# Eight unused columns behind each block of the sign weights

## The chip, the cores and the metric

The kernel runs on one core of a Trainium2 chip. The metric is the device time of one execution in microseconds; the time before is the median of three runs, 437.38 us (437.32 to 437.59).

## The reference

The input x is 2 sequences of 4096 vectors of 256 (fp32). A gated recurrence comes first, then a feed-forward layer with binarised weights; each is added to its input and followed by a layer norm.

```python
u = x @ W_in + b_in                       # 64 wide
g = sigmoid(x @ W_gate + b_gate)          # 256 wide
h_t = tanh(h_prev @ A + u_t @ Bm)         # a scan over 4096 steps
y_t = h_t @ C.T + u_t @ D.T
y_t = g_t * y_t + (1.0 - g_t) * x_t
x1 = layernorm(x + ys @ W_out + b_out + x)

alpha = mean(abs(w), axis=1, keepdims=True); bw = alpha * sign(w)
f = gelu(einsum('bsd,hd->bsh', x1, bw1) + b1)     # 1024 wide
out = layernorm(x1 + einsum('bsh,dh->bsd', f, bw2) + b2)
```

What matters here is the second half: both of its weight matrices are a sign (-1, 0 or 1) times one scale per row. The kernel multiplies by the signs alone and applies the scales afterwards.

## The kernel before, in words

The 8192 tokens are 16 chunks of 512 (`N`). The scan is cut into 64 segments that run side by side (`SEG`), so that a step of the recurrence is one small product `ps_s` (L157) and a tanh for all segments; these steps are strewn among the other work. The order of instructions on every engine is written out by hand (`manual_schedule`), and a running sum of costs (`emit`, `COST`) decides where a step of the recurrence is put in. The first 80 us or so hold the recurrence's input `u` (L131) and the first gates `ps_g` (L313); then comes the loop over chunks. In one round of the loop a chunk goes through its four `up` and four `down` parts, while chunks after it go through the gate, the mix `ps_y` (L374), the projection `ps_z` (L399) and the turning, and the chunk before it through the last layer norm.

The products that concern the change are two.

- `up` (L486): `ps_h`, 128 of the 1024 hidden units for 512 tokens. The weights that are loaded are a block of `sg1`, 128 columns for one of the two halves `k` of the 256 inputs and one of the eight blocks `j`; the moving operand is x1, split in two fp32r parts, `xhi` and `xlo`, of which each is 512 columns. Four matmuls make one `ps_h`, in the order (xhi, k=0), (xhi, k=1), (xlo, k=0), (xlo, k=1), all with the same j. There are 512 in a run.
- `down` (L528): `ps_o`, 128 tokens by 256 outputs. Here the loaded weights are 128 columns of the hidden layer, split into `hhi` and `hlo`, and the moving operand is block j of `sg2`, 256 columns. For one j there are eight matmuls in a row (four blocks of tokens, two parts). There are 1024 in a run, in the last chunk partly under the name `ps_p`.

Both are fp32r, one pass each. The other products are fp32: the trace shows two instructions for each of them. In the trace each matmul has a record of the weight load (PEld) and one of the product (PE).

`sg1` and `sg2` are made once, early in the kernel: `load_w` brings in the weights in four parts, `prepare_w` reduces them to scales, and `signs` writes the signs, on VectorE, with a comparison (L194) and a combination (L195) for each 512 columns. `signs` takes flat rows before the change. All tiles of the pool `const`, and then those of the other pools, lie one behind another in each partition, in the order in which they are asked for, so the sizes of `sg1` and `sg2` move what lies behind.

Of the kernel before, what the change touches and what calls it, by code (L numbers as in the profile page):

```python
# [8 lines left out]
FP = mybir.dt.float32  # L9
FR = mybir.dt.float32r  # L10
I32 = mybir.dt.int32
AF = mybir.ActivationFunctionType
ALU = mybir.AluOpType
# [3 lines left out]
P = 128  # L17
B, T, DM, S, H = 2, 4096, 256, 64, 1024
KD = DM // P
KH = H // P  # L20
# [3 lines left out]
N = 512  # L24
# [5 lines left out]
TOL = 2.0**-20  # L30
TGB = 9
XTB = 8
EARLY = 500
TOP, LOW = slice(0, S), slice(S, P)

# [2 lines left out]
def gated_recurrence_then_binary_ffn(  # L38
# [16 lines left out]
    nc = tc.nc  # L55

    cp = ctx.enter_context(tc.tile_pool(name="const", bufs=1))
    xp = ctx.enter_context(tc.tile_pool(name="xin", bufs=2))
    wk = ctx.enter_context(tc.tile_pool(name="work", bufs=2))
# [16 lines left out]
    cd = cp.tile([P, DM], FP, name="cd")  # L76
    w_gate = cp.tile([P, KD, DM], FP, name="w_gate")
    w_out = cp.tile([P, KD, DM], FP, name="w_out")
    sg1 = cp.tile([P, KD, H], FR, name="sg1")
    sg2 = cp.tile([P, KH, DM], FR, name="sg2")  # L80
    bias_c = cp.tile([P, 1 + KD + KH], FP, name="bias_c")
    bin_c = bias_c[:, 0:1]
    b1_c = bias_c[:, 1 + KD :]
# [16 lines left out]
    def load_xT(c, pieces=1):  # L100
        x_tiles[c] = xp.tile([P, KD, N], FP, tag="xt", name=f"xt{c}", bufs=XTB)
        for k in range(pieces):
            cut = slice(k * KD // pieces, (k + 1) * KD // pieces)
            nc.sync.dma_start(out=x_tiles[c][:, cut, :], in_=xT[c][:, cut, :])
# [19 lines left out]
    def u_of_chunks(*chunks):  # L124

        n = N * len(chunks) // 2
        parts = [(chunks[0], 0), (chunks[1], 0) if len(chunks) == 2 else (chunks[0], 1)]
        ps = p_1.tile([P, N], FP, tag="h", name=f"ps_u{chunks[0]}")
        for k in range(KD):
            for (c, i), r in zip(parts, (LOW, TOP)):  # L130
                nc.tensor.matmul(  # L131
                    ps[r, :n],
                    w_in[k],
                    x_tiles[c][:, k, bass.ts(i, n)],
                    start=k == 0,
                    stop=k == KD - 1,
                    skip_group_check=True,
                )
        for (c, i), r in zip(parts, (LOW, TOP)):
            to = u_of[:, bass.ds(c * SPC + i * n // W, n // W)].rearrange("p j b k -> p (j b k)")  # L140
            if r is TOP and c == FIRST:
                nc.scalar.activation(to, ps[r, :n], AF.Identity, bias=bin_c[r, :])
            else:
                nc.vector.tensor_scalar(to, ps[r, :n], bin_c[r, :], None, ALU.add)
        have_u.update(chunks)
        yield
# [42 lines left out]

    def signs(dst, src, nm):  # L190

        for i in range(2):
            neg = wk.tile([P, N], FP, tag="xlo", name=f"neg{nm}_{i}")
            nc.vector.tensor_scalar(neg, src[:, bass.ts(i, N)], 0.0, None, ALU.is_lt)  # L194
            nc.vector.scalar_tensor_tensor(  # L195
                dst[:, bass.ts(i, N)], src[:, bass.ts(i, N)], 0.0, neg, ALU.is_gt, ALU.subtract
            )

    w_tiles = {}
# [14 lines left out]
    def prepare_w(n):  # L214
        half = bass.ts(n % 2, KH // 2)
        t, t2 = w_tiles[n]
        if n < 2:
            nc.vector.tensor_reduce(al1[:, half], t2, AX.X, ALU.add, apply_absolute_value=True)
            nc.vector.tensor_scalar(al1[:, half], al1[:, half], 1.0 / DM, None, ALU.mult)
            signs(sg1[:, n, :], t, f"a{n}")  # L220
        else:
            nc.vector.tensor_reduce(
                al2[:, n % 2, :],
                t.rearrange("p j d -> p d j"),
                AX.X,
                ALU.add,
                apply_absolute_value=True,
            )
            if n == 3:
                nc.vector.tensor_add(al2[:, 0, :], al2[:, 0, :], al2[:, 1, :])  # L230
            signs(
                sg2[:, half, :].rearrange("p j d -> p (j d)"),
                t.rearrange("p j d -> p (j d)"),
                f"b{n}",
            )

    def mean_w2():
        ps = p_1.tile([P, N], FP, tag="h", name="ps_al2")
# [90 lines left out]
    class Chunk:  # L329
# [6 lines left out]
        def load_x(self):  # L336
            self.xt = xp.tile([P, KD, N], FP, tag="xt", name=f"xt_{self.nm}", bufs=XTB)
            nc.sync.dma_start(out=self.xt, in_=self.at(xT, self.c))
# [138 lines left out]
        def up(self, g, apart=False):  # L477
            nm = f"{self.nm}_{g}"
            h = wk.tile([P, 2, N], FP, tag="h", name=f"h{nm}")
            hi = wk.tile([P, 2, N], FR, tag="hhi", name=f"hhi{nm}", bufs=3)  # L480
            self.h[g] = h, hi
            for i in range(2):
                j = 2 * g + i
                ps = p_1.tile([P, N], FP, tag="h", name=f"ps_h{nm}_{i}")
                for n, (k, part) in enumerate((k, p) for p in (self.hi, self.lo) for k in range(KD)):
                    nc.tensor.matmul(  # L486
                        ps,
                        sg1[:, k, bass.ts(j, P)],
                        part[:, k, :],
                        start=n == 0,  # L490
                        stop=n == 2 * KD - 1,
                    )
                to = h[:, i, :]
                if self.far:
                    to = to.rearrange("p (i a c) -> p a i c", a=P // 32, c=32)
                nc.scalar.activation(  # L496
                    to,
                    ps.rearrange("p (a i c) -> p a i c", a=P // 32, c=32) if self.far else ps,
                    AF.Gelu,
                    bias=b1_c[:, j : j + 1],  # L500
                    scale=al1[:, j : j + 1],
                )
                if i == 1:
                    for part in range(2) if apart else [slice(0, 2)]:
                        nc.scalar.copy(hi[:, part, :], h[:, part, :])  # L505
                yield
# [18 lines left out]
        def down_part(self, j, tb):  # L525
            ps, i, first = self.banks[tb]
            for part in self.h[j // 2]:
                nc.tensor.matmul(  # L528
                    ps[:, i, :],
                    part[:, j % 2, bass.ts(tb, P)],  # L530
                    sg2[:, j, :],
                    start=j == 0 and part is self.h[j // 2][0] and first,
                    stop=j == KH - 1 and part is self.h[j // 2][1],
                    skip_group_check=True,
                )
# [128 lines left out]
    def emit(what, pieces, pace=5600):  # L664
        nonlocal since
        for _ in pieces:
            since += COST.get(what, 0)
            if since >= pace:
                since = min(since - pace, pace // 2)
                if ready():  # L670
                    next_steps()
# [21 lines left out]
    def parts(n, pace):  # L693
        emit("part", (next(early, None) for _ in range(n)), pace)

    ET = mybir.EngineType
    with tc.manual_schedule(engines={ET.PE, ET.Activation, ET.DVE, ET.Pool, ET.SP}):
# [8 lines left out]
        for n, pair in enumerate(pairs):  # L706
            before = 2 if n == 0 else 1
            parts(before, EARLY)
            if pair:
                emit("", u_of_chunks(*pair))  # L710
                if pair == (13, 14):
                    emit("", u_of_chunks(15, 0))
                emit("u", [None], EARLY)
            for c in loads[n]:
                load_xT(c)
            if n == 0:
                load_weights()
            if n == 3:
                halve_weights()
            if n >= 5:  # L720
                load_xT(n + 3)
                ch[n - 4].load_n()
                if n == 5:
                    ch[0].load_u()
                else:
                    ch[0].load_n()
                    ch[1].load_u()
                    ch[2].load_u()
            for i in range(7 - before):
                if 1 <= n < 5 and i == 0:  # L730
                    load_w(n - 1)
                if 2 <= n < 6 and i == 3:
                    prepare_w(n - 2)
                parts(1 if (n, i) != (6, 5) else 0, EARLY)
        assert done >= WARM + SPC, done
        emit("u", u_of_chunks(3), EARLY)
        for i in range(4):
# [191 lines left out]
```

## Time and profile before

| | |
|---|---|
| median of three runs | 437.38 us |
| the profiled execution | 437.67 us, its span 435.9 us |
| TensorE products (PE) | 425.5 us busy, 98% of the span, 2402 instructions |
| weight loads (PEld) | 344.3 us, 79% |
| VectorE | 332.4 us, 76% |
| ScalarE | 286.0 us, 66% |
| GpSimd | 155.8 us, 36% |
| `ps_h`, xhi and xlo | 256 + 256 matmuls, mean record 444 and 394 ns |
| `ps_o`, hhi and hlo | 496 + 496 matmuls, mean record 286 and 279 ns (32 more as `ps_p`) |
| granted TensorE clock | 0.994 of full speed |

A record of a matmul lasts from its start until its modelled end, and the records of neighbours overlap: the pace of TensorE is read from the distance between starts, or from the length of a piece in the chain of waits divided by its count, not from a record's length.

### The profile page before, as it was taken

What the parts mean: (1) busy time and instruction counts of PE and PEld (TensorE: products, weight loads), DVE (VectorE), ACT (ScalarE), POOL (GpSimd) and SP (SyncE); (2) the same over time, 40 slices, a digit from 0 to 9 for tenths busy, and PEclk for the clock granted to TensorE, in tenths of its full rate; (3) what the DMA queues carried; (4) which work ended last, traced back from release to release, by engine and by line L of the source; (5) the groups of instructions that cost most, each with busy time, mean ns of one, the idle gap of its engine ahead of it and who ended that gap; (6) DMA issues with size and microseconds to landing.
All of it is one profiled execution on the core that took longest, in us unless ns stands there. A gap on an engine that the chain in (4) does not pass through costs nothing.

```text
span 435.9 us, 6818 instructions
## 1 busy us (share of the span) xinstructions
PE 425.5 (98%) x2402; PEld 344.3 (79%) x2402; DVE 332.4 (76%) x569; ACT 286.0 (66%) x480; POOL 155.8 (36%) x176
## 2 busy tenths in 40 slices
PE   8999999999999999999999999999999999999992
PEld 5665767788888879797979797978888888888982
DVE  0245937895979798888888897979797979797674
ACT  2443452486587776767677776777767585849881
POOL 1000050474143435253525443444343444533413
PEclk9999999999999999999999999999999999999997
DMA  8877713400251615152426242534233232311102
GB/s 297 300 282 261 269 36 128 163 2 0 44 174 44 217 46 178 38 186 80 144 66 192 76 144 69 166 102 124 91 107 109 58 111 60 111 36 50 48 2 102
DMA packets 31479, 51.34 MB, mean 118 GB/s; under 512 B 5328, under 2 KB 19664, under 8 KB 31440
## 3 DMA queue, kind: packets, MB, share of 16 engines
q1 hardware_dynamic: 30864, 50.48, 36.4%
q8 instruction: 21, 0.34, 0.3%
q10 hardware_dynamic: 576, 0.37, 0.3%
q14 instruction: 18, 0.15, 0.1%
HBM read 31.43 MB, written 8.39 MB: 91 GB/s over the span
## 4 chain that ended last, share of the span: by engine, by line
PE 89%; DVE 5%; ACT 2%; DMA 1%; issue 1%; POOL 1%; SPq 0%; POOLq 0%; DVEq 0%
PE ps_h L486 25%; PE ps_o L528 25%; PE ps_g L313 12%; PE ps_z L399 11%; PE ps_y L374 6%; PE ps_s L157 6%; PE ps_u L131 3%; DMA xt<-in_xT 1%; DVE hlo L512 1%; ACT xn L278 1%; POOL rs_b L265 1%; PE ps_t L430 1%; DVE bs_b L255 1%; DVE d L381 1%; ACT h L496 1%
## 5 line engine op out<-in xcount | busy, mean ns | idle before, releaser
L528 PE MATMUL ps_o<-sg,hhi 128*128 128x256 f32 x496 | 121.4, 286 | 0.0
L528 PE MATMUL ps_o<-sg,hlo 128*128 128x256 f32 x496 | 117.9, 279 | 0.1
L496 ACT ACTIVATE h<-ps_h,bias_c,al 128x512 f32<-128x512 f32 x128 | 95.5, 771 | 16.8 <-PE ps_h L486 13.0
L528 PEld LDWEIGHTS ps_o<-sg,hhi 128*128 128x128 f32 x496 | 93.5, 189 | 1.1 <-DVE o L544 0.3
L528 PEld LDWEIGHTS ps_o<-sg,hlo 128*128 128x128 f32 x496 | 93.5, 188 | 1.1 <-DVE hlo L512 0.3
L486 PE MATMUL ps_h<-xhi,sg 128*128 128x512 f32 x256 | 92.9, 444 | 0.3 <-ACT h L496 0.3
L359 POOL TENSOR_TENSOR xn<-xn,bo_r 128x256 f32<-128x256 f32 x64 | 54.7, 888 | 88.6 <-DMA xn<-in_x 78.4
L512 DVE TENSOR_TENSOR hlo<-h,hhi 128x1024 fp32r<-128x1024 f32 (+1 forms) x65 | 79.5, 1240 | 5.0 <-ACT hhi L505 5.0
L486 PE MATMUL ps_h<-xlo,sg 128*128 128x512 f32 x256 | 80.1, 394 | 0.2
L265 POOL TENSOR_TENSOR rs_b<-rs_b,neg_half 128x4 f32<-128x4 f32 (+1 forms) x17 | 28.1, 1655 | 115.1 <-DVE rs_b L264 105.0
L505 ACT CAST hhi<-h 128x1024 fp32r<-128x1024 f32 (+1 forms) x65 | 67.4, 1039 | 2.0
L313 PE MATMUL ps_g<-xt,w_gate 128*128 128x384 f32 (+3 forms) x208 | 66.2, 430 | 0.1
L486 PEld LDWEIGHTS ps_h<-xhi,sg 128*128 128x128 f32 x256 | 46.5, 189 | 18.9 <-issue 11.7
L158 ACT ACTIVATE st<-ps_s 64x128 f32<-64x128 f32 x112 | 30.0, 268 | 45.7 <-PE ps_s L157 45.3
L486 PEld LDWEIGHTS ps_h<-xlo,sg 128*128 128x128 f32 x256 | 48.0, 188 | 11.9 <-DVE xlo L440 0.7
L157 PEld LDWEIGHTS ps_s<-st,wab 128*128 128x128 f32 x224 | 38.5, 189 | 21.6 <-ACT st L158 9.7
L359 POOL TENSOR_TENSOR xn<-xn,b_r 128x256 f32<-128x256 f32 x64 | 52.9, 855 | 1.1 <-PE ps_t L430 1.1
L399 PE MATMUL ps_z<-w_out,tg 128*128 128x256 f32 x224 | 50.6, 379 | 0.0
L399 PEld LDWEIGHTS ps_z<-w_out,tg 128*128 128x128 f32 x224 | 41.4, 190 | 5.1
L157 PE MATMUL ps_s<-st,wab 128*128 128x128 f32 x224 | 43.8, 277 | 0.1
L278 ACT ACTIVATE xn<-xn,nm_a,rs_a 128x256 f32<-128x256 f32 x60 | 31.2, 591 | 14.4 <-DVE nm_a L270 14.3
L265 POOL TENSOR_TENSOR rs_a<-rs_a,neg_half 128x4 f32<-128x4 f32 x16 | 17.2, 1072 | 65.0 <-DVE rs_a L264 63.0
(79 smaller groups left out, 481.5 us busy)
## 6 DMA issues: line engine op xcount, KB each, us to landing
xt<-in_xT SPq DMA_DIRECT2D x35, 512.0 KB, 4.4
xn<-in_x SPq DMA_DIRECT2D x16, 512.0 KB, 3.4
out_y<-xn SPq DMA_DIRECT2D x15, 512.0 KB, 2.6
xlo<-xb SPq DMA_DIRECT2D x208, 32.0 KB, 1.9
hu<-st SPq DMA_DIRECT2D x32, 128.0 KB, 2.3
w1t<-in_w1T SPq DMA_DIRECT2D x2, 512.0 KB, 4.9
w1n<-in_w SPq DMA_DIRECT2D x2, 512.0 KB, 6.1
w2t<-in_w2T SPq DMA_DIRECT2D x2, 512.0 KB, 5.2
```

Source lines behind the costliest of these rows:

```text
L157: nc.tensor.matmul(p_h, ab, st[:, j].rearrange("p b k -> p (b k)"), start=True, stop=True)
L158: nc.scalar.activation(h_of[:, j + 1].rearrange("p b k -> p (b k)"), p_h[TOP, :], AF.Tanh)
L265: nc.gpsimd.tensor_tensor(rs, rs, neg_half[:, cut], ALU.pow)
L278: nc.scalar.activation(r, r, AF.Identity, bias=self.sh[:, i : i + 1], scale=rs)
L313: nc.tensor.matmul(ps[:, cut], w_gate[:, k, bass.ts(m, P)], xt_[:, k, cut], start=k == 0 and i == 0, stop=k == KD - 1, skip_group_check=True,)
L359: nc.gpsimd.tensor_tensor(r[:, i, :], r[:, i, :], row, ALU.add)
L399: nc.tensor.matmul(self.ps_z[:, i, :], self.y[:, k, bass.ts(i, P)], w_out[:, k, :], start=k == 0, stop=k == KD - 1,)
L486: nc.tensor.matmul(ps, sg1[:, k, bass.ts(j, P)], part[:, k, :], start=n == 0, stop=n == 2 * KD - 1,)
L496: nc.scalar.activation(to, ps.rearrange("p (a i c) -> p a i c", a=P // 32, c=32) if self.far else ps, AF.Gelu, bias=b1_c[:, j : j + 1], sc ...
L505: nc.scalar.copy(hi[:, part, :], h[:, part, :])
L512: nc.vector.tensor_sub(lo[:, i, :], h[:, i, :], hi[:, i, :].bitcast(FP))
L528: nc.tensor.matmul(ps[:, i, :], part[:, j % 2, bass.ts(tb, P)], sg2[:, j, :], start=j == 0 and part is self.h[j // 2][0] and first, stop=j ...
```

## The change

Each block of the sign weights gets eight unused fp32r columns (32 bytes) behind it. `sg1` becomes a tile of 2 x 8 blocks of 136 columns, of which 128 are used, and `sg2` one of 8 blocks of 264 columns, of which 256 are used. In each partition a block of `sg1` follows the last after 544 bytes instead of 512, a block of `sg2` after 1056 instead of 1024. `signs` gets its operands in blocks instead of flat rows. The products read the same columns as before.

```diff
+GAP = 8
-    sg1 = cp.tile([P, KD, H], FR, name="sg1")
-    sg2 = cp.tile([P, KH, DM], FR, name="sg2")
+    sg1 = cp.tile([P, KD, KH, P + GAP], FR, name="sg1")
+    sg2 = cp.tile([P, KH, DM + GAP], FR, name="sg2")
...
     def signs(dst, src, nm):
+        half = src.shape[1] // 2
         for i in range(2):
-            neg = wk.tile([P, N], FP, tag="xlo", name=f"neg{nm}_{i}")
-            nc.vector.tensor_scalar(neg, src[:, bass.ts(i, N)], 0.0, None, ALU.is_lt)
+            part = src[:, bass.ts(i, half), :]
+            neg = wk.tile([P, half, src.shape[2]], FP, tag="xlo", name=f"neg{nm}_{i}")
+            nc.vector.tensor_scalar(neg, part, 0.0, None, ALU.is_lt)
             nc.vector.scalar_tensor_tensor(
-                dst[:, bass.ts(i, N)], src[:, bass.ts(i, N)], 0.0, neg, ALU.is_gt, ALU.subtract
+                dst[:, bass.ts(i, half), : src.shape[2]], part, 0.0, neg, ALU.is_gt, ALU.subtract
             )
...
-            signs(sg1[:, n, :], t, f"a{n}")
+            signs(sg1[:, n], t.rearrange("p (j c) -> p j c", c=P), f"a{n}")
...
-            signs(
-                sg2[:, half, :].rearrange("p j d -> p (j d)"),
-                t.rearrange("p j d -> p (j d)"),
-                f"b{n}",
-            )
+            signs(sg2[:, half], t, f"b{n}")
...
-                        sg1[:, k, bass.ts(j, P)],
+                        sg1[:, k, j, :P],
...
-                    sg2[:, j, :],
+                    sg2[:, j, :DM],
```

## The prediction

> **What bounds the kernel now.** I read the page's first part, then busy time by stretches of 40 us, then the chain of waits in the steady part, then the starts of single matmuls. The page says how full TensorE is:
>
> ```profile
> PE 425.5 (98%) x2402; PEld 344.3 (79%) x2402; DVE 332.4 (76%) x569; ACT 286.0 (66%) x480; POOL 155.8 (36%) x176
> ```
>
> The stretches (columns: PE, PEld, DVE, ACT, POOL busy us, granted clock, DMA share, GB/s) say that it waits for nobody between about 80 and 400 us:
>
> ```profile
> 200.00:240.00 40.00, 40.00 (x230) 33.83 (x230) 33.94 (x62) 28.30 (x44) 16.50 (x18) 1.00 0.40 119
> 240.00:280.00 40.00, 40.00 (x227) 33.19 (x226) 34.31 (x54) 28.28 (x45) 17.39 (x18) 1.00 0.33 93
> ```
>
> TensorE is full, the clock is granted whole, VectorE (34 of 40 us) and ScalarE (28 of 40) have room. A nanosecond on or off a TensorE instruction there is one on or off the end. A full engine can still be slow at each instruction, so the next view is the chain, start and length of each piece:
>
> ```profile
> 202.96 1.72 PE ps_g L313 x4
> 204.67 1.84 PE ps_h L486 x8
> 206.52 0.22 PE ps_s L157 x2
> 206.74 1.83 PE ps_o L528 x16
> 208.57 3.45 PE ps_z L399 x16
> ...
> 217.97 1.89 PE ps_o L528 x16
> 219.86 1.72 PE ps_y L374 x4
> ```
>
> Divide length by count. fp32 products: ps_z 3.45/16 = 216 ns for 256 columns, ps_y and ps_g 1.72/4 = 430 ns for 512, both 0.84 ns per column. The fp32r products with the sign weights: ps_h 1.84/8 = 230 ns for 512 columns and ps_o 1.83/16 = 114 ns for 256, both 0.45 ns per column. Were fp32r just twice as fast per column, these would be 215 and 108 ns. So the two lines that the change touches, and only they, carry a surplus of about 15 and 6 ns. And ps_o has two speeds: one piece of 16 took 1.83 us, another 1.89. Starts of single matmuls inside these two pieces:
>
> ```profile
> 214.29 0.28 PE L528 MATMUL ps_o<-sg,hlo 128*128 128x256 f32 x1
> ...
> 215.65 0.28 PE L528 MATMUL ps_o<-sg,hlo 128*128 128x256 f32 x1
> ...
> 218.17 0.28 PE L528 MATMUL ps_o<-sg,hlo 128*128 128x256 f32 x1
> ...
> 219.58 0.28 PE L528 MATMUL ps_o<-sg,hlo 128*128 128x256 f32 x1
> ```
>
> Twelve matmuls lie between the first and second line, (215.65-214.29)/12 = 113.3 ns each, and twelve between the third and fourth, (219.58-218.17)/12 = 117.5 ns. Same instruction, same shape, same places modulo 256 bytes; only the moment at which the run began differs. Taken one by one over the trace, ps_o steps by 113 to 119 ns, mean 115.3; ps_h steps by 226, 229 and 232 ns in turn, at some places 235, mean 229.9. Such steady, repeating steps don't look like disturbance by VectorE or ScalarE, whose work moves about; they look like two streams of TensorE itself (the moving operand and the next weights) meeting in a fixed rhythm.
>
> **What the Trainium skill says.** "TensorE: Matmul & The Clock Gate", Back-to-back issue gap, gives N/2.4 + 2.5 ns: 215.8 ns for 512 columns and 109.2 for 256. This trace agrees for ps_z's passes (216 ns), and not for ps_h (230) and ps_o (113 to 118). "SBUF — State Buffer", Who interferes with whom, gives TensorE two independent read ports and says "PE and ACT never wait on anyone." Taken strictly the change does nothing; the two speeds of ps_o, equal in everything but phase, speak against taking it strictly. Its Specifications name lines of 16 bytes; the new steps (544 and 1056 bytes) are whole lines, so no block begins inside one.
>
> **The change part by part.**
> 1. Places. In both built programs sg1 begins at byte 128 modulo 256 of a partition, and sg2 too. Now a block of sg1 is 512 bytes and of sg2 1024, so all blocks stay at 128. With the gap the steps are 544 = 2x256+32 and 1056 = 4x256+32, so block j lies at 128+32j modulo 256. The other operand (xhi/xlo for ps_h, hhi/hlo for ps_o) begins at 192 in both programs: all tiles behind the weights move by 512+256 = 768 bytes, three times 256. So now the distance between the stream and the load beside it is always 64 bytes, one way for ps_h (weights are loaded), the other for ps_o (signs are streamed). Afterwards it takes all eight multiples of 32, changing with j: every 4 matmuls in ps_h, every 8 in ps_o.
> 2. TensorE's counts, order, waits, columns: unchanged, 512 ps_h and 1024 ps_o (the tail's ps_p included). No wait, DMA or semaphore is added.
> 3. VectorE's signs: eight comparisons (median 420 ns) and eight combinations (691 ns, output fp32r) now see 3-D patterns, the second with a gap in its output. No row shows such an output, so bounds: nothing, or doubled, which is 8x0.42+8x0.69 = 8.9 us more VectorE work in 30 to 56 us. I take nothing. Even the upper end is covered: VectorE is busy 26.1 of 40 us in 40 to 80, and the first reader of sg1 is at 85.9 us, of sg2 at 93.9. Without that cover, u's evictions behind them on VectorE would come late, and the recurrence's steps with them; I allow 1 us for that in the range.
>
> So all hangs on the price of one matmul at the eight distances, of which the trace shows one distance for each product. Bounds from the gain side: no surplus at all, 512x(229.9-215.8) = 7.2 us and 1024x(115.3-109.2) = 6.2 us, together 13.4 us. From what recurs in the trace: if every product ran at the fastest steady rate seen, 512x(229.9-226) = 2.0 and 1024x(115.3-113.3) = 2.0, together 4.0 us less. If every one ran at the slowest, 512x(235-229.9) = 2.6 and 1024x(118-115.3) = 2.8, together 5.4 us more.
>
> **The forecast.** I take the 4.0 us: a rhythm that today can settle into its slow form for whole runs is broken at every new j, and few distances should be worse than one at which surplus is already 14 ns. This is a choice of sign more than a measurement. The profiled execution has span 435.9 and 437.67 us in all, 1.8 outside the span; 435.9-4.0 = 431.9, plus 1.8 is 433.7, and the median of the runs is 0.3 below the profiled one: 433.4 us. What would be late next: VectorE's load goes from 85% to 86% of the steady part, so nothing takes the gain back.
>
> **The rivals.**
> - *The surplus goes almost wholly* (9 us or more): the stream and the load collide only at distances near 64. For it: the fp32 products, which stream at half the rate, show no surplus. Against: three other distances in eight would have to be harmless in both directions. 437.4-9 = 428.4, at the limit 424.0 us.
> - *Slower*: block j = 2 lands at 192, where the other operand begins, so stream and load start level, which never happens now. If equal places are the bad ones, j = 1, 2, 3 pay. With three blocks in eight paying the present surplus twice, 3/8 of 13.4 = +5.0 us, 442.4; the slowest recurring rates give +5.4, 442.8. It decides as soon as the mean surplus over eight distances exceeds today's 14.1 ns in ps_h plus twice 6.1 in ps_o. For it: ps_o's fast form, 113.3, is already near the 110 ns of ps_s (0.22/2), which also loads weights every time, so part of today's rhythm is a good one that turning would break. Against: today's mean is far from good in ps_h.
> - *No effect*: the surplus belongs to fp32r's stream, or the load runs past all places anyhow, wherever it starts: 437.4. For it: the skill's sentence, and that a load of 512 bytes passes each place modulo 256 twice. Against: the two speeds.
>
> **Numbers.** A measurement of this kernel tells about 0.2% (0.9 us) from no change. Chances: about 4 us faster 0.46, nearly all gone 0.10, no effect 0.08, slower 0.36. So faster 0.56, same 0.08, slower 0.36. Range: 429.0 leaves 0.10 below it, and 442.6 leaves 0.10 above (the bad places costing more than twice, VectorE's microsecond). The likeliest case alone spans 429 to 436.5.
>
> **What would show it.** Right: the chain's pieces ps_h x8 nearer 1.80 than 1.84 us and ps_o x16 at 1.81 or less, different by j, with ps_z, ps_y and ps_g unchanged and the same wait table. Slower: pieces with j near 2 longest, above 1.88 and 1.89 us. No effect: the steps of 226, 229, 232 and 113.3 stand as they are. If the fp32 pieces or TensorE's waits move instead, the cause is elsewhere (what VectorE wrote late, or where the other tiles went) and the reasoning is wrong even with the right number.

## The result and the profile after

The changed kernel takes 441.51 us (median of three runs, 441.26 to 441.65) against 437.38: ratio 1.0093, 95% interval 1.0070 to 1.0115. It is slower by 4.1 us where 4.0 us less was forecast. The profiled execution of it took 441.26 us, its span is 439.4 us, 3.5 more than before.

The page's first part and the busy time by stretches of 40 us (PE, PEld, DVE, ACT, POOL busy us, clock, DMA share, GB/s) of the changed kernel:

```profile
PE 428.9 (98%) x2402; PEld 347.6 (79%) x2402; DVE 329.0 (75%) x569; ACT 286.2 (65%) x480; POOL 148.5 (34%) x176
...
200.00:240.00 40.00, 40.00 (x227) 33.58 (x226) 33.74 (x57) 28.09 (x45) 14.76 (x17) 1.00 0.38 109
240.00:280.00 40.00, 40.00 (x226) 33.08 (x225) 33.27 (x58) 28.60 (x45) 16.09 (x16) 1.00 0.33 96
```

TensorE is as full as before and waits for nobody; its 2402 records take 3.4 us longer, 428.9 against 425.5. In the same 80 us it starts 453 matmuls instead of 457. The chain of waits (start, length, piece) shows which ones are slow:

```profile
202.52 1.91 PE ps_o L527 x16
204.43 1.72 PE ps_g L312 x4
206.14 1.86 PE ps_h L485 x8
208.00 0.22 PE ps_s L158 x2
208.22 1.87 PE ps_o L527 x16
210.09 3.45 PE ps_z L398 x16
```

ps_g, ps_s and ps_z have their old lengths to the hundredth. ps_h went from 1.83 to 1.85 us for 8 to 1.85 or 1.86, ps_o from 1.83 (sometimes 1.89) to between 1.87 and 1.91 for 16. From the starts of single matmuls over the whole trace: ps_o's mean step is 118.2 ns (115.3 before), ps_h's 232.2 (229.9). Added up over the two traces, start by start, the steps inside ps_o grew by 2.46 us, those inside ps_h by 0.75, and those between one of the two and another product by 0.27, together 3.5 us: the growth of the span in these two traces. (Multiplying the mean steps by 1024 and 512 would give 4.2; that is too much, because the longer first step of a run, which these means leave out, did not grow with the others.) Instruction by instruction against the trace of before, the lag grows from 0.1 us at the first ps_h to 3.6 us at the last matmul; there is no place where it jumps.

One run of sixteen in the changed kernel, with j=0 in its first eight matmuls (the old place) and j=1 in the last eight (32 bytes on); columns are start and length of a record:

```profile
208.64 0.28 PE L527 MATMUL ps_o<-sg,hlo 128*128 128x256 f32 x1
...
208.98 0.28 PE L527 MATMUL ps_o<-sg,hhi 128*128 128x256 f32 x1
209.10 0.28 PE L527 MATMUL ps_o<-sg,hlo 128*128 128x256 f32 x1
...
209.80 0.28 PE L527 MATMUL ps_o<-sg,hlo 128*128 128x256 f32 x1
```

Three steps lie between the first two lines, 0.34/3 = 113 ns, the fast rhythm of before. From the next block on it is gone: six steps between the last two, 0.70/6 = 117 ns, single ones up to 122. In this run the old place has the old pace and the new place a slower one. The same holds over the trace of the changed kernel as far as the fast rhythm goes: the block j=0, on the old place, has it in 12 of 16 runs, and no later block has it in any run.

### The profile page after: what moved, and what is told of

It is laid out like the page before. It is cut to its first block, busy times and chain, and to the rows that moved or that the text cites. A ratio compares the mean times of both kernels' runs of the same rounds, so it can differ in the third digit from the quotient of the medians.

```text
span 439.4 us, 6818 instructions
## 1 busy us (share of the span) xinstructions
PE 428.9 (98%) x2402; PEld 347.6 (79%) x2402; DVE 329.0 (75%) x569; ACT 286.2 (65%) x480; POOL 148.5 (34%) x176
## 4 chain that ended last, share of the span: by engine, by line
PE 91%; DVE 5%; ACT 1%; DMA 1%; POOL 1%; issue 0%; SPq 0%; POOLq 0%; DVEq 0%
PE ps_h L485 26%; PE ps_o L527 25%; PE ps_g L312 12%; PE ps_z L398 11%; PE ps_y L373 6%; PE ps_s L158 6%; PE ps_u L132 3%; DMA w_gate<-in_W_gate 1%; ACT xn L277 1%; PE ps_p L527 1%; DVE hlo L511 1%; POOL rs_b L264 1%; PE ps_t L429 1%; DVE bs_b L254 1%; DVE d L380 1%; DVE o L543 0%
## 5 line engine op out<-in xcount | busy, mean ns | idle before, releaser
L527 PE MATMUL ps_o<-sg,hhi 128*128 128x256 f32 x496 | 123.8, 288 | 0.0
L527 PE MATMUL ps_o<-sg,hlo 128*128 128x256 f32 x496 | 120.5, 282 | 0.0
L358 POOL TENSOR_TENSOR xn<-xn,bo_r 128x256 f32<-128x256 f32 x64 | 48.5, 794 | 86.0 <-DMA xn<-in_x 80.4
L358 POOL TENSOR_TENSOR xn<-xn,b_r 128x256 f32<-128x256 f32 x64 | 51.7, 838 | 1.1 <-PE ps_t L429 1.1
```

Of the source, the lines that this page charges most:

```text
L358: nc.gpsimd.tensor_tensor(r[:, i, :], r[:, i, :], row, ALU.add)
L527: nc.tensor.matmul(ps[:, i, :], part[:, j % 2, bass.ts(tb, P)], sg2[:, j, :DM], start=j == 0 and part is self.h[j // 2][0] and first, stop ...
```

## The experiments

Three theories were set against each other. **Distance**: a product's pace depends on where its weight load begins relative to the moving stream, modulo 256 bytes; the kernel before has a cheap distance, and turning (going from one distance to the next with j) averages over cheap and dear ones. **Turning**: what costs is the change of place from block to block, which breaks a rhythm. **Alignment**: a block must begin on a multiple of 64 or 128 bytes. "Distance" below is the load's place minus the stream's, modulo 256; before it is 64 in ps_o and 192 in ps_h.

**One gap at a time.** gap_sg1 keeps sg2 as before, gap_sg2 keeps sg1 as before; signs is that of the changed kernel in both.

```diff
 # gap_sg1
-    sg2 = cp.tile([P, KH, DM + GAP], FR, name="sg2")
+    sg2 = cp.tile([P, KH, DM], FR, name="sg2")
 # gap_sg2
-    sg1 = cp.tile([P, KD, KH, P + GAP], FR, name="sg1")
+    sg1 = cp.tile([P, KD, KH, P], FR, name="sg1")
```

> The gap behind sg1's blocks alone. All three theories put the loss where the matmuls are, so this run only shares it out: in the changed kernel the steps inside ps_h grew by 0.75 us in all, inside ps_o by 2.46 us. Expected 0.7 to 1.1 us slower than before (438.1 to 438.5), ps_h's mean step near 232.3 ns instead of 229.9, ps_o's unchanged at 115.3.

> The gap behind sg2's blocks alone: expected 2.5 to 3.4 us slower than before (439.9 to 440.8), ps_o's mean step near 118.1 to 118.5 ns, ps_h's unchanged at 229.9. If the two gaps together cost clearly less or more than one by one, something besides the two products is at work.

gap_sg2: 440.10 us against 437.81, ratio 1.0058 (1.0041 to 1.0075), ps_o 117.9, ps_h 229.9: near the lower end of what was expected. gap_sg1: 440.29 us, ratio 1.0060 (1.0043 to 1.0077), 2.5 us and more than expected. Its ps_h is 232.8 as thought, but its ps_o, whose places are untouched, is 116.2. The chain of gap_sg1 shows why:

```profile
208.00 1.83 PE ps_o L527 x16
...
215.36 1.89 PE ps_o L527 x16
```

The fast and the slow form of before are both there, but the slow one (1.89) comes more often: before, of the runs after a step of the recurrence only those of j=4 were slow, here most of those of j=2 and j=6. Over the whole trace 18 of 61 runs are slow before and 35 here. What a run follows matters even in the kernel before: with j=0 all 11 runs after a step of the recurrence are fast, and three of the five that follow ps_h directly are slow. The likely reading is that ps_h's pace changes the moment at which a run of ps_o begins, and with it the form into which it settles; no run changes that moment alone. So the two parts are not independent. Their losses, 2.5 and 2.3, come to 0.7 us more than the 4.1 of both, which is within the intervals.

**Places held fixed, 128 bytes on, and everything moved by 32.** const_128 has no gap; all blocks of both weights begin 128 bytes later, and filler keeps every other tile at its place modulo 256. all_32 puts 32 bytes ahead of sg1, so that the weights and all tiles behind them move together.

```diff
 # const_N: OFF = N/4 columns
-    sg1 = cp.tile([P, KD, H], FR, name="sg1")
+    sg1_w = cp.tile([P, 64 + KD * H], FR, name="sg1")
+    sg1 = sg1_w[:, OFF : OFF + KD * H].rearrange("p (k h) -> p k h", k=KD)
 # sg2 in the same way
 # all_32
+    sg1_w = cp.tile([P, 8 + KD * H], FR, name="sg1")
+    sg1 = sg1_w[:, 8:].rearrange("p (k h) -> p k h", k=KD)
```

> No gap: every block of both sign weights begins 128 bytes later modulo 256, the same for all blocks, everything else at its old place modulo 256. Distance theory (each product's pace depends on where the load begins relative to the stream, and the kernel before happens to have a cheap distance): as the changed kernel's blocks at these distances, ps_o near 118.0 ns (load 192 after the stream) and ps_h near 231.1 (load 64 after), so about 2.8 + 0.6 = 3.4 us slower, 440.8. Turning theory (the cost is the change of place from block to block): no change, 437.4. Alignment theory (a block must begin on a multiple of 64 or 128 bytes): no change, 437.4.

> No gap: sg1, sg2 and all tiles behind them begin 32 bytes later, so that load and stream keep their distance, but no block begins on a multiple of 64 any more. Distance theory: no change, 437.4, ps_h 229.9 and ps_o 115.3 ns. Turning theory: no change. Alignment theory: a loss like the changed kernel's, 3 to 4 us.

all_32: 437.45 us against 437.81, ratio 0.9992 (0.9983 to 1.0001), ps_o 115.0, ps_h 229.6. Its chain has no slow piece among the runs of ps_o in the stretch:

```profile
206.69 1.84 PE ps_o L530 x16
208.54 3.45 PE ps_z L401 x16
...
217.94 1.85 PE ps_o L530 x16
```

Nothing is lost although no block begins on a multiple of 64 any more: alignment to 64 or 128 bytes is out, and it speaks for the place against the other operand's and not a block's own place. It is one joint move, though, and not all stayed as it was: only 3 of 61 runs of ps_o settle in the slow form (18 before), while the first steps of those in the fast form take longer, 1.84 or 1.85 us a run instead of 1.83. So the own place may still have a part in how a run begins.

const_128: 439.45 us, ratio 1.0035 (1.0021 to 1.0049), which fits none of the theories as stated. ps_h is slower with a fixed place (233.2), so distance counts there without any turning. ps_o has the two forms of before, 30 runs fast and 31 slow. Its mean of 115.8 lies between those of the three kernels that keep the old distance (115.0 in all_32, 115.3 before, 116.2 in gap_sg1), so 192 is no worse a distance than 64. The changed kernel's blocks at this very distance step by 118.0, so for ps_o something besides the distance counts too.

**Turning between two cheap places.** 64 and 192 are both cheap for ps_o when held. alt_128 changes between them from block to block, with a gap of 32 columns behind sg2's blocks (`GAP = 32`, sg1 as before).

> A gap of 32 columns (128 bytes) behind sg2's blocks alone: even blocks stay at the old place, odd blocks lie 128 bytes on, modulo 256. Each of the two places was cheap when all blocks had it (ps_o 115.3 and 115.8 ns). Turning theory (a change of place from block to block breaks the fixed rhythm of ps_o into which a run of matmuls settles): ps_o near 117.5 to 118.5 ns and 2.3 to 3.2 us slower, with the break at the ninth matmul of each run of sixteen. Distance theory (each block at the pace of its own distance): ps_o near 115.5 ns, 0 to 0.3 us. ps_h 229.9 in both.

439.58 us against 437.84, ratio 1.0040 (1.0025 to 1.0054), 1.7 us and less than the 2.3 to 3.2 expected; ps_o 117.4, ps_h 230.2. Turning by itself costs: 117.4 is 1.9 ns above the mean of the two places held (115.3 and 115.8), and 1.2 above the slowest kernel that holds one of them (gap_sg1, 116.2). One of its runs of sixteen, from its timeline of TensorE:

```profile
215.34 0.28 PE L527 MATMUL ps_o<-sg,hhi 128*128 128x256 f32 x1
...
215.68 0.28 PE L527 MATMUL ps_o<-sg,hlo 128*128 128x256 f32 x1
215.80 0.28 PE L527 MATMUL ps_o<-sg,hhi 128*128 128x256 f32 x1
...
216.62 0.28 PE L527 MATMUL ps_o<-sg,hlo 128*128 128x256 f32 x1
```

Up to the eighth matmul 0.34/3 = 113 ns; from the ninth, the first at the other place, 0.82/7 = 117 ns until the end of the run. Of the 61 runs only 15 begin like this one, and all 15 lose the fast rhythm at the second block; the other 46 are slow from the start, though their first block lies at the old place. Its chain has both sorts:

```profile
207.63 1.89 PE ps_o L527 x16
...
215.04 1.86 PE ps_o L527 x16
```

So turning goes with the loss of the fast rhythm, but a break in mid-run is the smaller part of it; why most runs begin slow here is not shown.

**The other fixed distances.** As const_128, by N bytes.

> No gap; all sign blocks 64 bytes later modulo 256, so that load and stream begin at the same place in both products. Distance theory for ps_o: 118.5 ns, as the changed kernel's blocks there; turning theory: a settled run, 113.3 or 117.5 ns, mean 114 to 117.5. ps_h by distance: 231 to 234 ns, the place of the changed kernel's j = 2; by turning: 229.9. My rival of the forecast (level starts are the bad place) wants both clearly above the rest, 236 and 121 ns.

> No gap; all sign blocks 192 bytes later modulo 256: load and stream half a turn apart in both products. Distance theory: ps_o 119.3, ps_h 232 to 233.6 ns, about 5 us slower. Turning theory: ps_o settles at 113.3 or 117.5, mean 114 to 117.5, ps_h 229.9; 437.4 to 439.6.

> No gap; all sign blocks 224 bytes later (32 earlier) modulo 256. Distance theory: ps_o 118.3, ps_h 232.5 ns, about 4.4 us slower. Turning theory: ps_o 114 to 117.5, ps_h 229.9. With const_64, const_128 and const_192 this says whether ps_h, which a change of place every four matmuls hits less, goes by distance when ps_o does not: then ps_h 231 to 234 and ps_o below 117.5.

> No gap; all sign blocks 96 bytes later modulo 256. ps_o has the same steady pace at distances 64 and 192, and at 0 and 128, so far: its dependence may repeat every 128 bytes. Then this distance (load 224 after the stream) equals that of the blocks 224 later (96): 118.2 ns. ps_h does not repeat (229.9 at load 192 after the stream, 233.2 at 64), its value here lies between 231 and 234. Time 440.5 to 441.8.

> No gap; all sign blocks 32 bytes later modulo 256: the seventh of the eight distances, at a place held for the whole run. ps_o (load 32 after the stream): 117.0 to 119.0 ns; ps_h (load 224 after): 231 to 234 ns. Time 440 to 442. If the changed kernel's paces are the means over the eight fixed distances (distance theory, with turning as a small addition in ps_o alone), this run and the next have to bring these means to about 117.8 ns for ps_o and 232.2 for ps_h, against 118.2 and 232.2 measured in the changed kernel.

> No gap; all sign blocks 160 bytes later modulo 256, the eighth distance. ps_o (load 160 after the stream): 117.5 to 120 ns, equal to const_32's if ps_o repeats every 128 bytes; ps_h (load 96 after): 231 to 234 ns. Time 440 to 442.5.

One timed execution each (const_128: the median of five), so a time has no interval; 16 executions of the kernel before, in the series of const_128, lay between 437.37 and 438.60. The mean steps are over some 900 and 400 matmuls of a trace; the longer first steps of a run are left out.

| shift, bytes | us | ps_o distance | ps_o ns | ps_h distance | ps_h ns |
|---|---|---|---|---|---|
| 0 (before) | 437.4 | 64 | 115.3 | 192 | 229.9 |
| 32 | 441.71 | 32 | 118.2 | 224 | 233.3 |
| 64 | 441.80 | 0 | 119.6 | 0 | 231.2 |
| 96 | 439.79 | 224 | 117.0 | 32 | 232.8 |
| 128 | 439.45 | 192 | 115.8 | 64 | 233.2 |
| 160 | 443.06 | 160 | 120.0 | 96 | 234.3 |
| 192 | 442.15 | 128 | 119.4 | 128 | 232.2 |
| 224 | 441.43 | 96 | 118.2 | 160 | 233.6 |
| mean | 440.9 | | 117.9 | | 232.6 |
| changed kernel | 441.51 | each in turn | 118.2 | each in turn | 232.2 |

All seven others are slower than before. ps_o is slower at six of the seven distances, 192 being the exception; ps_h is slower at six too, while at 0 its longer steps (231.2) are nearly made up by shorter first ones, and the sum of its steps over the trace is only 0.1 us more. Turning alone would have left ps_o at 117.5 or less and ps_h at 229.9 in kernels that hold every place, so it cannot be the whole cause. The mean of the eight fixed kernels, 117.9 and 232.6 ns, nearly gives the changed kernel's 118.2 and 232.2. At the six distances other than 64 and 192 no run of ps_o is in the fast rhythm. ps_h, which moves in these kernels too, is not the reason: in gap_sg1, where it steps by 232.8, 26 of 61 runs of ps_o are fast. The chain of const_64:

```profile
202.66 1.91 PE ps_o L532 x16
204.57 1.72 PE ps_g L317 x4
206.29 1.86 PE ps_h L490 x8
...
208.37 1.91 PE ps_o L532 x16
210.28 3.46 PE ps_z L403 x16
```

and that of const_128, where runs are at 1.82 or, as some before, at 1.89:

```profile
207.46 1.82 PE ps_o L532 x16
209.28 3.45 PE ps_z L403 x16
212.74 1.87 PE ps_h L490 x8
214.60 0.22 PE ps_s L161 x2
214.82 1.89 PE ps_o L532 x16
```

In const_64 a settled ps_o steps by 120 ns throughout, in const_192 mostly by 119 and 121 in turn, at the other four slow distances in longer cycles.
My expectation that ps_o would repeat every 128 bytes failed: it holds within half a nanosecond for 64/192 and 0/128, and not for 96/224 (118.2, 117.0) or 32/160 (118.2, 120.0). The rival's bad place, level starts in both products, isn't borne out either: distance 0 is among the dear ones for ps_o but, after that of before, the cheapest of the eight for ps_h.

**Half steps.**

> No gap; all sign blocks 16 bytes later modulo 256. Both distances then lie a half step beside those of before (load 48 after the stream in ps_o, 80 before it rounded to 48 before in ps_h). If the pace depends on whole steps of 32 bytes, as before: ps_o 115.3, ps_h 229.9, 437.4. If it changes smoothly, ps_o 116 to 118 and ps_h 230 to 232, 439 to 440. A pace below that of before would point to a faster version.

> No gap; all sign blocks 240 bytes later, that is 16 earlier, modulo 256: the half step on the other side. Same two readings: 437.4 with whole steps, 439 to 440 with a smooth dependence; a pace below that of before would point to a faster version.

441.86 us for 16 bytes later (ps_o 118.9 at distance 48, ps_h 232.4 at 208) and 440.83 for 16 earlier (ps_o 119.0 at 80, ps_h 230.3 at 176), beside 437.67 for the kernel before; one execution each. The cheap place of ps_o is narrow: 16 bytes to either side cost it some 3.6 ns. ps_h loses 2.5 ns on one side and next to nothing on the other. Neither whole steps of 32 bytes nor a smooth run between them fits ps_o. No distance tried is better than that of before, so there was no faster version to run.

## Why the prediction was wrong

**What bounds the kernel: right.** What TensorE's steps grew by came through to the end: 3.5 us of steps and 3.5 us of span in the changed kernel, and in every other run the span grew by what its ps_o and ps_h steps grew, within 0.7 us (of which up to 0.5 arose before the first ps_h).

**Places and counts (parts 1 and 2): right.** Counts and order of matmuls are the same, 2402 in both traces, and only the two products with sign weights changed their pace. That places count modulo 256 was assumed and is still not tested.

**VectorE's signs (part 3): right at the lower bound.** The group of combinations in the changed kernel (minimum, median, maximum in ns) is what it was:

```profile
L198 DVE SCALAR_TENSOR_TENSOR sg<-w1t,nega x4: 693/693/693, 30.4 to 40.4; 128x512 fp32r<-128x512 f32 x4
L198 DVE SCALAR_TENSOR_TENSOR sg<-w2t,negb x4: 691/692/1099, 49.4 to 54.9; 128x512 fp32r<-128x512 f32 x4
```

**The forecast's choice: wrong, and it is the step that failed.** It said that "few distances should be worse than one at which surplus is already 14 ns". All seven other kernels are worse, by 1.6 to 5.3 us against the kernel before in the same series: a surplus of 14 ns in ps_h and 6 in ps_o is the least of the eight distances, not a bad draw. With each place held, the mean over the eight is 117.9 ns for ps_o and 232.6 for ps_h, above the 115.3 and 229.9 of before, where the forecast put the changed kernel at 113.3 and 226. I read the surplus against the fp32 products as a sign that the place was poor; it only says that fp32r matmuls with a load beside them don't reach half the fp32 time at any place tried. The other half of the argument was the wrong way round. I said that turning would break the slow rhythm; in ps_o it is the fast one, 113.3 ns, that is not found after a change of place, in none of 61 runs of alt_128.

**The size: too large even with the sign right.** The 4.0 us took 226 ns as a steady rate of ps_h. It is one step of the cycle 226, 229, 232, whose mean is 229; and a run of ps_o in its fast form has slower first steps too. An estimate from the trace of before: ps_h at 229 gains 512x0.9 = 0.5 us, and the 18 runs of ps_o in the slow form gain, at 1.83 instead of 1.89 us each, 18x0.06 = 1.1 us, together 1.6 us.

**The rivals.** "Slower" had the deciding point right (the mean surplus over eight distances exceeds today's) and nearly the size, +5.0 to +5.4 against +4.1. That the size came near was luck, for the mechanism behind it was not borne out: dear places don't gather around level starts. "No effect" fell with gap_sg1, gap_sg2 and the fixed distances. In the means the distances explain nearly all of the loss (117.9 of 118.2, and more than all of ps_h's). That agreement is one of means: in ps_o four of the changed kernel's eight kinds of block run 1.1 to 2.3 ns off the pace of their own distance held fixed (at 192, 118.0 against 115.8; at 0, 118.5 against 119.6). And alt_128 loses 1.9 ns by turning alone. So both have a part, and how ps_o's 2.9 ns divide between them is not shown.

**What the skill said.** "SBUF — State Buffer", Who interferes with whom, has it that "PE and ACT never wait on anyone." TensorE may not wait for another engine there, but the places of what it reads are not indifferent: ps_o takes 115.3 or 120.0 ns with nothing changed but where the sign blocks lie. The measurement decides. The formula of "TensorE: Matmul & The Clock Gate", Back-to-back issue gap, was also put to a use that the section does not give it: there it is the gap of an isolated matmul, and in a stream of weight loads and matmuls the spacing is set by both. So the "no surplus at all" of the bounds was not a pace that the page promises for ps_h and ps_o. Nor does ps_z agree with it as the prediction says: 216 ns is what the formula gives for 512 columns, and an instruction of ps_z has 256, for which it gives 109.2. It would fit if an fp32 instruction went over its columns twice, which no run here shows.

**Open.** Which structure of the memory or of TensorE makes the two streams meet, why 64 and 192 have a fast rhythm in ps_o, what decides the form in which a run begins, and whether 256 bytes is the period of the distances (no run moved a weight by 256 alone). That it is these two streams is inferred: moved together by 32 bytes they keep their pace, moved against each other they lose it.

## What to carry to other kernels

A difference between the measured pace and an ideal one says that there is a price, not that another place is cheaper: hold each place fixed in a kernel of its own, read the steps between starts in the trace, and then choose the best. Rotating over all places gave about their mean here (118.2 and 232.2 ns against 117.9 and 232.6). Where TensorE is full, an innocent change in a tile's size can shift operands against each other and move the time by one per cent, 16 bytes being enough; after any such change compare the pieces' lengths per instruction, not busy shares.

## What the runs showed of the hardware that was not expected

- The pace of an fp32r matmul beside the next weight load depends on the two operands' places in a partition: ps_o (256 columns) 115.3 to 120.0 ns, ps_h (512 columns) 229.9 to 234.3 ns over eight distances. Moving both operands by 32 bytes changes the time by nothing measurable (ratio 0.9992); moving one by 16 changes ps_o to 118.9.
- The same stream of matmuls at the same distance has two steady paces, 113.3 and 117.5 ns, at distances 64 and 192. A run settles in its first steps and then keeps its pace to the end of its sixteen matmuls; with a change of place at the ninth (alt_128) none ended in the fast one.
- The fp32 products keep their pace in all these runs, ps_z 3.45 or 3.46 us for 16 in every chain shown. Only all_32 tests them, since there alone their operands move against each other, by 32 bytes (`w_out` lies ahead of the weights, `tg` behind): the mean step of ps_z is 215.7 ns in the kernel before and in all_32. Other distances were not tried.
